# Routed experts in a graph network: edge rows gathered in sixteen blocks by destination, and shares of 13 of 25 node tiles made beside the experts

## The chip, the cores and the metric

The kernel runs on one core of a Trainium2 chip. A core has five engines with a queue each: PE (TensorE, matrix products), DVE (VectorE, elementwise work and reductions), ACT (ScalarE, activation functions), POOL (GpSimd, here mostly the issue of gathers and scatters) and SP (SyncE, plain transfers). Each queue runs in order. Sixteen DMA engines carry the transfers. The metric is the time of one execution in microseconds (us), as the median of several. Times inside the execution are counted from the start of the profiled span.

## What is computed

The program is a stack of graph layers on 3125 nodes with 256 features and edge lists of up to 50000 edges. The change lies in one of them, a feed-forward layer of four experts whose gates come from graph attention. Cut to what matters (M nodes, D=256, 4 heads, 4 experts):

```
h = (x @ W_gat).reshape(M, HEADS, NUM_EXPERTS)
src = concatenate([edge_index[0], loops]); dst = concatenate([edge_index[1], loops])
a_src = (h * att_src).sum(-1); a_dst = (h * att_dst).sum(-1)
e = leaky_relu(a_src[src] + a_dst[dst], negative_slope=0.2)
ee = exp(e - segment_max(e, dst)[dst])
alpha = ee / (segment_sum(ee, dst)[dst] + 1e-16)
agg = segment_sum(h[src] * alpha[:, :, None], dst).reshape(M, 16) + b_gat
scores = layernorm(agg).reshape(M, HEADS, NUM_EXPERTS).mean(1)
topk_s, topk_i = top_k(scores, 2); w = softmax(topk_s)
for ei in range(NUM_EXPERTS):
    g = where(topk_i == ei, w, 0).sum(-1)
    out += g[..., None] * (gelu(x @ W1[ei] + b1[ei]) @ W2[ei] + b2[ei])
```

Here the experts need only `x`, while the gates need, for every node, the rows of all nodes that point at it. There are 32768 such edges, and no node has more than 40 of them.

## The kernel before

**Sizes.** The 3125 nodes are padded to 3200, that is 25 tiles of 128, one node to a partition. `GE` is 32768 edges, `GT` = 256 groups of 128, `GK` = 40 rows fetched per node.

**The survey** (`survey`, L63 to L207) runs first. It counts each node's edges (`gcnt`), and where its run in the sorted list of edges begins (`gstart_i`). It sums up faults (`sv_fault`, five columns) to one number, `bad`. The whole body is built twice: with `bad` at 0 the arm with a plan runs, otherwise a general arm. An early stage of the body then sorts the source numbers of the edges by destination into a list in HBM, `gsorted`.

**The layer** (`routed_layer_in_order`, from L1204) does the following.

1. `router_nodes` normalizes the nodes, makes `xt` (the transposed, normalized nodes), `hg` (the 16 values of W_gat) and the two sides `a_src`, `a_dst`. A table `nodes` with 20 numbers per node (4 of `a_src`, 16 of `hg`) goes to HBM by SP (L1219).
2. On POOL's queue, 256 indirect gathers (helper line L236) fetch the 20 numbers of the source of 128 edges each: `ge<-nodes,src_parts`. The list is laid out with 256 consecutive edges to a partition. Eight tiles of 32 gathers each are written back to HBM as the table `edges`, sorted by destination (L1232). A gather here is a DMA that POOL issues.
3. In five parts of five node tiles, `shares` fetches for each node 40 consecutive rows of `edges`, 80 bytes each (`el<-edges,gstart_i`, one gather for a tile of 128 nodes, 410 KB). Then come the arithmetic of the attention on DVE (L1253 to L1271) and one exp on ACT (L1261). Rows beyond a node's own are pushed to minus infinity by the mask `off` (L1257). The results are `gat_num` and `gat_den`. The buffers `el` and `gat_s` are two each.
4. Beside that, `routed_experts` (L1190) runs 4 experts over 7 chunks of columns, six of 512 and one of 128, written (e, c) below with both counted from 0. A chunk has four pairs of `l0f_ph` product (L1200, two passes of k each) and gelu (L1201, ACT). Then `keep` makes the second product `l0f_po` (L576, in `project`; two node tiles to a PSUM tile) and `put` (L1288, DVE), which adds the bias and frees the PSUM tile. Results of experts 1 to 3 go to HBM through SP (L1290).
5. `router_gates` begins with the `ag` tensor_tensor (L1121), which needs every `gat_num`. The gates weigh the experts' results into X, and the next layer follows.

**What sets the order.** The body is written as a program for a scheduling framework. It puts each engine's instructions in a fixed order and inserts semaphore waits where a tile's or a table's data demand them. `tc.issue_after(x)` puts the instructions within behind x on their engine. `keep` calls `shares(5 * k, put.ins, last.ins)` at the chunks (3,2) to (3,6) of the last expert. DVE's part of the share stands behind the chunk's last `put`, and ACT's exp behind its last gelu. A read of `edges` waits for the writes to it that stand ahead of it, and a later write to it waits for such reads. A tile from a pool of two buffers waits until the one before the last is no longer used.

Of the kernel before, what the change touches and what calls it, by code (L numbers as in the profile page):

```python
# [7 lines left out]
F32 = mybir.dt.float32  # L8
BF16 = mybir.dt.bfloat16
I32 = mybir.dt.int32  # L10
AF = mybir.ActivationFunctionType
OP = mybir.AluOpType
AX = mybir.AxisListType
# [3 lines left out]
P = 128  # L17
N = 3125
NT = 25
# [5 lines left out]
GE = 32768  # L25
GT = GE // P
# [4 lines left out]
NEG = -1.0e30  # L31
# [7 lines left out]
SLOT = P  # L39
GO = 8  # L40
GK = 40


def bcast_rows(ap, width):
# [17 lines left out]
def survey(ctx, tc, A):  # L62
# [9 lines left out]
    with ExitStack() as st:  # L72
# [67 lines left out]
            d0, d1 = WKS.index(k), NT - WKS[::-1].index(k)  # L140
            V.tensor_scalar(first[:, d0:d1], begin[:, d0:d1], row_at[k], None, op0=OP.add)

        fault = sp.tile([P, 5], F32, name="sv_fault")
        V.memset(fault, 0.0)
        V.tensor_tensor(junk, nxt, ids["dst"], op=OP.is_lt)
        V.tensor_reduce(fault[:, 0:1], junk, axis=AX.X, op=OP.max)
        b = sp.tile([P, NT + 1], F32, name="sv_b")
# [42 lines left out]
        V.tensor_tensor(same, far, ids["dst"], op=OP.is_equal)  # L190
        V.scalar_tensor_tensor(same, ids["dst"], float(N), same, op0=OP.is_lt, op1=OP.mult)
        V.tensor_reduce(fault[:, 4:5], same, axis=AX.X, op=OP.max)
        faults = ps.tile([1, 5], F32, name="sv_faults")
        T.matmul(faults, ones[:, :1], fault, start=True, stop=True)
        total = sp.tile([1, 1], F32, name="sv_total")
        V.tensor_reduce(total, faults, axis=AX.X, op=OP.add)
# [13 lines left out]
def body(ctx, tc, A, out, plan):  # L210
# [12 lines left out]
    def load(stack_pool, ap, shape, name, dtype=F32, **kw):  # L223
        t = stack_pool.tile(shape, dtype, name=name, **kw)
        nc.sync.dma_start(t, ap)
        return t
# [8 lines left out]
    def gather(dst, table, idx):  # L235
        return G.indirect_dma_start(out=dst, out_offset=None, in_=table, in_offset=bass.IndirectOffsetOnAxis(ap=idx, axis=0))  # L236
# [967 lines left out]
    def routed_layer_in_order():  # L1204

        with ExitStack() as st:
            open_stage(st)
            sp = pool(st, "l0f")
            gate = sp.tile([P, NT, 4], F32, name="gate")
            ytab = [dram.tile([P, NT, D], F32, name=f"l0f_y{e}") for e in range(4)]  # L1210
            b1 = load(sp, A["l0_ffn_b1"], [P, 16], "l0f_b1")
            with ExitStack() as st2:
                ga = pool(st2, "gat")
                xt, hg, a_src, a_dst = router_nodes(st2, ga)
                node = ga.tile([P, NT, 20], F32, name="node")
                V.tensor_copy(node[:, :, :4], a_src)
                V.tensor_copy(node[:, :, 4:], hg)
                nodes = dram.tile([NP, 20], F32, name="nodes")
                nc.sync.dma_start(nodes[:, :].rearrange("(t p) w -> p t w", p=P), node)  # L1219
                part = load(ga, gsorted[:, :].rearrange("(p j) o -> p (j o)", p=P), [P, GT], "src_parts", I32)  # L1220
                edges = dram.tile([GE + GK, 20], F32, name="edges")
                pad = ga.tile([GK, 20], F32, name="edges_pad")
                V.memset(pad, 0.0)
                nc.sync.dma_start(edges[GE:, :], pad)
                by_part = edges[:GE, :].rearrange("(p j) w -> p j w", p=P)
                gx = pool(st2, "gat_e", 2)
                for j0 in range(0, GT, 32):
                    ge = gx.tile([P, 32, 20], F32, name="ge")
                    for j in range(32):
                        gather(ge[:, j, :], nodes[:, :], part[:, j0 + j : j0 + j + 1])  # L1230

                    G.dma_start(by_part[:, j0 : j0 + 32, :], ge)  # L1232

                num = ga.tile([P, NT, 16], F32, name="gat_num")
                den_ = ga.tile([P, NT, 4], F32, name="gat_den")
                top = ga.tile([P, 5, 4], F32, name="gat_top")


                off = ga.tile([P, NT, GK + 1], F32, name="gat_off")
                V.tensor_tensor(  # L1240
                    off, iota_f[:, None, : GK + 1].to_broadcast([P, NT, GK + 1]), plan["gcnt"][:, :, None].to_broadcast([P, NT, GK + 1]), op=OP.is_ge
                )
                V.tensor_scalar(off, off, NEG, None, op0=OP.mult)
                V.memset(off[:, :, GK:], 0.0)

                def shares(d0, dve, act):

                    el = gx.tile([P, 5, GK + 1, 20], F32, name="el")
                    ds_ = slice(d0, d0 + 5)
                    for i in range(5):  # L1250
                        gather(el[:, i, :GK, :].rearrange("p k w -> p (k w)"), edges[:, :], gstart_i[:, d0 + i : d0 + i + 1])
                    with tc.issue_after(dve):
                        V.tensor_copy(el[:, :, GK, :], node[:, ds_, :])  # L1253
                        s = gx.tile([P, 5, GK + 1, 4], F32, name="gat_s")
                        V.tensor_tensor(s, el[:, :, :, :4], a_dst[:, ds_, None, :].to_broadcast([P, 5, GK + 1, 4]), op=OP.add)
                        V.scalar_tensor_tensor(s, s, 0.2, s, op0=OP.mult, op1=OP.max)
                        V.tensor_tensor(s, s, off[:, ds_, :, None].to_broadcast([P, 5, GK + 1, 4]), op=OP.add)  # L1257
                        V.tensor_reduce(top, s.rearrange("p d k h -> p d h k"), axis=AX.X, op=OP.max)
                        V.tensor_tensor(s, s, top[:, :, None, :].to_broadcast([P, 5, GK + 1, 4]), op=OP.subtract)
                    with tc.issue_after(act):  # L1260
                        S.activation(s, s, AF.Exp)  # L1261
                    V.tensor_reduce(den_[:, ds_, :], s.rearrange("p d k h -> p d h k"), axis=AX.X, op=OP.add)
                    vals = el.rearrange("p d k w -> p (d k) w")[:, :, 4:].rearrange("p e (h c) -> p e h c", h=4)
                    V.tensor_tensor(
                        vals, vals, s.rearrange("p d k h -> p (d k) h")[:, :, :, None].to_broadcast([P, 5 * (GK + 1), 4, 4]), op=OP.mult
                    )

                    for k in (20, 10, 5):
                        V.tensor_tensor(el[:, :, :k, 4:], el[:, :, :k, 4:], el[:, :, k : 2 * k, 4:], op=OP.add)
                    V.tensor_tensor(el[:, :, 0, 4:], el[:, :, 0, 4:], el[:, :, GK, 4:], op=OP.add)  # L1270
                    V.tensor_reduce(num[:, ds_, :], el[:, :, :5, 4:].rearrange("p d k w -> p d w k"), axis=AX.X, op=OP.add)  # L1271


                wp = pool(st2, "l0f_w", 2)
                ps = pool(st2, "l0f_ps", 2, PSUM)
                b2s = {}

                def keep(e, c, cl, ht, w2, last):
                    if e not in b2s:
                        b2s[e] = load(wp, bcast_rows(A["L0_ffn_b2"][e], D), [P, D], "l0f_b2")  # L1280
                    t0, n = c // P, cl // P
                    ys = y_first[:, t0 : t0 + n, :] if e == 0 else wp.tile([P, 4, D], F32, name="l0f_ys")[:, :n]
                    for j in range(0, n, 2):
                        m = min(2, n - j)
                        po = ps.tile([P, 2, D], F32, name="l0f_po")
                        for i in range(m):
                            project(po[:, i, :], ht, w2, j + i)
                        put = V.tensor_tensor(ys[:, j : j + m, :], po[:, :m, :], b2s[e][:, None, :].to_broadcast([P, m, D]), op=OP.add)  # L1288
                    if e:
                        nc.sync.dma_start(ytab[e][:, t0 : t0 + n, :], ys)  # L1290

                    k = c // 512 - 2
                    if e == 3 and k >= 0:
                        shares(5 * k, put.ins, last.ins)

                y_first = stage[0].tile([P, NT, D], F32, name="l0f_y_first", tag="xn")
                routed_experts(wp, ps, b1, xt, keep)
                router_gates(ga, gate, num.rearrange("p t (h c) -> p t h c", h=4), den_)
            with ExitStack() as st2:
                yp = pool(st2, "l0f_yp", 3)  # L1300
                for t in range(NT):
                    V.scalar_tensor_tensor(X[:, t, :], y_first[:, t, :], gate[:, t, :1], X[:, t, :], op0=OP.mult, op1=OP.add)
                for t0 in range(0, NT, 4):
                    n = min(4, NT - t0)
                    for e in range(1, 4):
                        y = yp.tile([P, 4, D], F32, name=f"l0f_yr{e}")
                        nc.sync.dma_start(y[:, :n], ytab[e][:, t0 : t0 + n, :])
                        for j in range(n):
                            t = t0 + j
                            V.scalar_tensor_tensor(X[:, t, :], y[:, j, :], gate[:, t, e : e + 1], X[:, t, :], op0=OP.mult, op1=OP.add)  # L1310
# [954 lines left out]
```

## Time and profile before

| | |
|---|---|
| median of 3 runs | 4866.56 us (4864.06 to 4866.61) |
| profiled execution | 4865.58 us, span 4863.8 us |
| granted PE clock, mean | 0.900 |
| PE, DVE, ACT, POOL busy | 83%, 47%, 24%, 32% of the span |
| first and last `ge` gather issued | 840.56, 1163.28 |
| first `el` gather issued | 1168.93 |
| PE at a standstill | 1143.1 to 1187.69 |
| first share's first sum on DVE | 1178.87 |
| `ag` starts | 1265.67 |

In a line of the timeline the first number is the start, the second the duration, then follow engine, line, operation and operands. In brackets stands how long the engine had been idle before, and which event is taken to have ended that. A line of the waits gives who waited at which line, for whom, the total in us, how often, and the longest. The 25 `el` gathers took:

```profile
L236 POOL DMA_INDIRECT el<-edges,gstart_i x25: 940/942/1770, 1168.9 to 1239.2; - x25
```

The three figures are minimum, median and maximum in ns, then the first and last start in us.

### The profile page before, as it was taken

The page shows a single profiled execution, that of the slowest core. Times are in us where ns is not written, and L with a number is a line of the kernel's source. Part 1 is how long each engine was busy: PE and PEld are TensorE (multiplying, and loading weights), DVE is VectorE, ACT ScalarE, POOL GpSimd, SP SyncE. Part 2 cuts the span into 40 slices and gives each one's busy share as a digit, 9 for nine tenths or more (in the row PEclk, how much of TensorE's full clock was granted, in tenths as well). Part 3 has the DMA queues.
Part 4 walks back from the last instruction along what each step waited for, and adds up shares of the span by engine and source line. Part 5 has one row for each costly group of instructions (what it writes and reads, how often), then busy time and mean ns, then how long its engine had stood idle before and what let it go on. Part 6 is the DMA issues. An engine that isn't in the chain of part 4 may idle for free. (4 is left out here: it accounts for less than half of the span.)

```text
span 4863.8 us, 54448 instructions
## 1 busy us (share of the span) xinstructions
PE 4053.8 (83%) x20057; PEld 2505.6 (52%) x20057; DVE 2280.8 (47%) x6284; ACT 1169.4 (24%) x2820; POOL 1545.1 (32%) x1497
## 2 busy tenths in 40 slices
PE   2488888996099996777689999899999997969987
PEld 2355544664067665555565555444444454634555
DVE  8986443113932337777669997600101033250143
ACT  0167721221021223444312223300102011110021
POOL 2077640775000017777406777200000002200010
PEclk6688889998599997888899999999999998989998
DMA  1046582122523347777614432022221322344200
GB/s 56 10 160 197 192 271 60 39 67 83 168 100 128 133 155 211 206 205 207 188 53 136 149 120 70 3 88 82 70 85 66 95 96 80 91 143 156 82 22 27
DMA packets 286833, 553.40 MB, mean 114 GB/s; under 512 B 81979, under 2 KB 195148, under 8 KB 275676
## 3 DMA queue, kind: packets, MB, share of 16 engines
q1 hardware_dynamic: 215804, 411.42, 25.1%
q0 software_dynamic: 70752, 138.40, 10.7%
q8 instruction: 160, 2.62, 0.2%
q14 instruction: 117, 0.96, 0.1%
HBM read 377.47 MB, written 172.20 MB: 113 GB/s over the span
## 5 line engine op out<-in xcount | busy, mean ns | idle before, releaser
L558 PE MATMUL agg_ps<-tt,h_l 128*128 128x512 bf16 (+3 forms) x3850 | 888.8, 395 | 51.5 <-ACT h_l L2045 44.4
L236 POOL DMA_INDIRECT h_kv<-kv_tab,kv_row x416 | 421.1, 1012 | 189.4 <-issue 65.8
L558 PEld LDWEIGHTS <-h_l 128*128 128x128 bf16 x3150 | 291.5, 98 | 333.4 <-issue 19.5
L239 POOL DMA_INDIRECT wgt_cells<-cw_wsum,cw_to x391 | 392.6, 1004 | 171.1 <-issue 111.6
L239 POOL DMA_INDIRECT gsorted<-gs_i,gpos x256 | 320.4, 1251 | 260.1 <-DVE gpos L909 173.7
L1642 PE MATMUL h_pq<-h_q,h_odt 128*128 128x256 bf16 x1248 | 213.8, 333 | 154.4 <-DVE h_qk L1644 154.2
L236 POOL DMA_INDIRECT ge<-nodes,src_parts x256 | 241.8, 945 | 234.6 <-PE l0f_po L576 156.9
L1842 DVE TENSOR_TENSOR at<-agg_ps,rdeg_r 128x512 f32<-128x512 f32 (+1 forms) x42 | 25.6, 633 | 589.1 <-PE agg_ps L558 589.1
L1962 POOL IOTA trash_slot<- 128x32 f32 x1 | 0.2, 158 | 877.8 <-PE l2g_ph L1861 877.8
L1787 ACT ACTIVATE l1f_h<-l1f_ph,bn_shift,bn_scale 128x512 f32<-128x512 f32 (+1 forms) x224 | 162.7, 731 | 387.2 <-PE l1f_ph L1784 387.2
L1642 PEld LDWEIGHTS <-h_odt 128*128 128x128 bf16 x1248 | 140.8, 116 | 209.8 <-issue 159.1
L558 PEld LDWEIGHTS agg_ps<-tt,h_l 128*128 128x128 f32 x700 | 126.5, 192 | 189.9 <-issue 188.9
L576 PE MATMUL l0f_po<-l0f_w,l0f_ht 128*128 128x256 f32 x800 | 179.8, 382 | 44.6 <-ACT l0f_ht L1201 44.6
L465 PE MATMUL pt<-ident,xn 128*128 128x128 f32 x300 | 64.4, 376 | 180.0 <-DVE xn L456 134.8
L576 PE MATMUL l1f_po<-l1f_Wo,l1f_h 128*128 128x256 f32 x800 | 204.4, 388 | 2.4 <-DVE X L1793 1.2
L1862 ACT ACTIVATE ht_next<-l2g_ph,l_bhid 128x512 f32<-128x512 f32 (+1 forms) x42 | 26.9, 641 | 717.0 <-PE l2g_ph L1861 717.0
L1784 PE MATMUL l1f_ph<-l1f_h,l1f_W 128*128 128x512 f32 (+1 forms) x448 | 195.5, 559 | 1.2 <-ACT l1f_h L1787 0.6
L1693 PE MATMUL h_po<-h_kv,h_of 128*128 128x256 f32 x832 | 189.7, 387 | 7.7 <-DVE h_kv L1689 4.1
L1784 PE MATMUL l1f_ph<-xt,l1f_W 128*128 128x512 f32 (+1 forms) x448 | 191.3, 547 | 1.1 <-issue 1.1
L576 PEld LDWEIGHTS l0f_po<-l0f_w,l0f_ht 128*128 128x128 f32 x800 | 152.9, 192 | 76.2 <-ACT l0f_ht L1201 45.4
L576 PEld LDWEIGHTS l1f_po<-l1f_Wo,l1f_h 128*128 128x128 f32 x800 | 146.1, 190 | 84.3 <-issue 28.3
L1200 PE MATMUL l0f_ph<-xt,l0f_w 128*128 128x512 f32 (+1 forms) x448 | 178.8, 549 | 3.0 <-ACT l0f_ht L1201 2.1
(628 smaller groups left out, 7460.5 us busy)
## 6 DMA issues: line engine op xcount, KB each, us to landing
tt<-cnt_ds SPq DMA_DIRECT2D x90, 640.0 KB
kv_tab<-kv SPq DMA_DIRECT2D x50, 1024.0 KB
tt<-wgt_cells SPq DMA_DIRECT2D x30, 1280.0 KB
wgt_cells<-cw_zero SPq DMA_DIRECT2D x6, 5800.0 KB
cw_row<-cell_r SPq DMA_DIRECT2D x23, 1128.0 KB
cw_ew<-in_ew_r_dram SPq DMA_DIRECT2D x22, 1108.0 KB
cnt_ds<-row_ds SPq DMA_DIRECT2D x150, 128.0 KB
cnt_sd<-cols SPq DMA_DIRECT2D x6, 3200.0 KB
```

Source lines behind the costliest of these rows:

```text
L236: return G.indirect_dma_start(out=dst, out_offset=None, in_=table, in_offset=bass.IndirectOffsetOnAxis(ap=idx, axis=0))
L239: G.indirect_dma_start(out=table, out_offset=bass.IndirectOffsetOnAxis(ap=idx, axis=0), in_=src, in_offset=None, **kw)
L465: T.transpose(pt[:, j, :], src[:, g + j, h * P : (h + 1) * P], ident)
L558: T.matmul(acc[h][:, :width], part[:, s, h * P : (h + 1) * P], tt[:, s - s0, :width], start=(s == 0 and i == 0), stop=(s == NT - 1 and i = ...
L576: T.matmul(psum, lhs[:, i, t * P : (t + 1) * P], rhs[:, i, :], start=(i == 0), stop=(bias is None and i == k - 1))
L1200: T.matmul(ph[:, :cl], w1[:, k, f * P : (f + 1) * P], xt[:, k, c : c + cl], start=(k == 0), stop=(k == 1))
L1642: T.matmul(pq[:, j, :], w["odt"][:, k0 + j, :], w["q3"][:, part, :], start=(part == 0), stop=(part == 2))
L1693: T.matmul(po, of[:, j, :], kv[:, j, D:], start=(k0 + j == 0), stop=(k0 + j == K - 1))
L1784: T.matmul(ph[:, :cl], ws[layer][:, k, o * P : (o + 1) * P], src[:, k, at : at + cl], start=(k == 0), stop=(k == 1))
L1787: S.activation(dst[:, o, :cl], ph[:, :cl], AF.Relu, bias=shi[:, col], scale=sca[:, col])
L1842: V.tensor_tensor(at[:, hf, c : c + cl], psum, rdeg_r[:, c : c + cl], op=OP.mult)
L1862: S.activation(nt_[:, o, c : c + cl], ph[:, :cl], AF.Relu, bias=b_hid[:, o : o + 1])
```

## The change

The 256 groups of edges are divided into `GB` = 16 blocks of 16, each of consecutive destinations: block b holds edges 2048b to 2048b+2047, 16 to a partition. The list of sources is loaded in that layout, in runs of 64 bytes. Each block is written to `edges` on its own (16 writes of 128x320 in place of 8 of 128x640). The node tiles are divided into six parts of 5, 5, 3, 5, 5 and 2 tiles; `GPARTS` gives for each the first tile, the number of tiles, and how many blocks are to be in `edges` before the part's rows are fetched.

A generator, `rows_of_edges`, issues for each part the gathers of its blocks, their writes, and the part's `el` gathers. Two parts are issued ahead of the experts, one more after each call of `shares`. `shares` is called at the chunks (1,4), (2,4), (3,1), (3,4), (3,5) and (3,6).

The table `edges` is filled with zeros first (a memset of 128x1280 and one SP transfer of 2.6 MB). The mask is made for all tiles at once with `a_dst` added in (`off`, 4100 numbers per partition), and each share has one operation less (L1257 is gone). The survey checks that the edges of the first parts do not reach past their blocks: three more columns of faults, three memsets, a matmul, three reductions and one comparison.

```diff
--- before.py
+++ after.py
@@ -39,6 +39,8 @@
 SLOT = P
 GO = 8
 GK = 40
+GB = 16
+GPARTS = [(0, 5, 6), (5, 5, 11), (10, 3, 14), (13, 5, GB), (18, 5, GB), (23, 2, GB)]
 
 
 def bcast_rows(ap, width):
@@ -140,8 +142,11 @@
             d0, d1 = WKS.index(k), NT - WKS[::-1].index(k)
             V.tensor_scalar(first[:, d0:d1], begin[:, d0:d1], row_at[k], None, op0=OP.add)
 
-        fault = sp.tile([P, 5], F32, name="sv_fault")
+        fault = sp.tile([P, 8], F32, name="sv_fault")
         V.memset(fault, 0.0)
+        ready = sp.tile([1, 3], F32, name="sv_ready")
+        for i, (_, _, b) in enumerate(GPARTS[:3]):
+            V.memset(ready[:, i : i + 1], float(b * GE // GB - GK))
         V.tensor_tensor(junk, nxt, ids["dst"], op=OP.is_lt)
         V.tensor_reduce(fault[:, 0:1], junk, axis=AX.X, op=OP.max)
         b = sp.tile([P, NT + 1], F32, name="sv_b")
@@ -190,7 +195,14 @@
         V.tensor_tensor(same, far, ids["dst"], op=OP.is_equal)
         V.scalar_tensor_tensor(same, ids["dst"], float(N), same, op0=OP.is_lt, op1=OP.mult)
         V.tensor_reduce(fault[:, 4:5], same, axis=AX.X, op=OP.max)
-        faults = ps.tile([1, 5], F32, name="sv_faults")
+
+        total_g = ps.tile([1, NT], F32, name="sv_total_g")
+        T.matmul(total_g, ones[:, :1], gcnt, start=True, stop=True)
+        upto_g = sp.tile([1, 3], F32, name="sv_upto_g")
+        for i, (d0, n, _) in enumerate(GPARTS[:3]):
+            V.tensor_reduce(upto_g[:, i : i + 1], total_g[:, : d0 + n], axis=AX.X, op=OP.add)
+        V.tensor_tensor(fault[:1, 5:8], upto_g, ready, op=OP.is_gt)
+        faults = ps.tile([1, 8], F32, name="sv_faults")
         T.matmul(faults, ones[:, :1], fault, start=True, stop=True)
         total = sp.tile([1, 1], F32, name="sv_total")
         V.tensor_reduce(total, faults, axis=AX.X, op=OP.add)
@@ -1217,52 +1229,78 @@
                 V.tensor_copy(node[:, :, 4:], hg)
                 nodes = dram.tile([NP, 20], F32, name="nodes")
                 nc.sync.dma_start(nodes[:, :].rearrange("(t p) w -> p t w", p=P), node)
-                part = load(ga, gsorted[:, :].rearrange("(p j) o -> p (j o)", p=P), [P, GT], "src_parts", I32)
+
+                per = GT // GB
+                part = ga.tile([P, GB, per], I32, name="src_parts")
+                nc.sync.dma_start(part, gsorted[:, :].rearrange("(b p j) o -> p b (j o)", p=P, b=GB))
                 edges = dram.tile([GE + GK, 20], F32, name="edges")
                 pad = ga.tile([GK, 20], F32, name="edges_pad")
                 V.memset(pad, 0.0)
                 nc.sync.dma_start(edges[GE:, :], pad)
-                by_part = edges[:GE, :].rearrange("(p j) w -> p j w", p=P)
+                by_block = edges[:GE, :].rearrange("(b p j) w -> b p j w", p=P, b=GB)
                 gx = pool(st2, "gat_e", 2)
-                for j0 in range(0, GT, 32):
-                    ge = gx.tile([P, 32, 20], F32, name="ge")
-                    for j in range(32):
-                        gather(ge[:, j, :], nodes[:, :], part[:, j0 + j : j0 + j + 1])
-
-                    G.dma_start(by_part[:, j0 : j0 + 32, :], ge)
+                fetched = []
+
+                def rows_of_edges():
+
+                    done = 0
+                    for d0, n, upto_block in GPARTS:
+                        for b in range(done, upto_block):
+                            ge = gx.tile([P, per, 20], F32, name="ge")
+                            for j in range(per):
+                                gather(ge[:, j, :], nodes[:, :], part[:, b, j : j + 1])
+
+                            G.dma_start(by_block[b], ge)
+                        done = upto_block
+                        el = gx.tile([P, 5, GK + 1, 20], F32, name="el")
+                        for d in range(n):
+                            gather(el[:, d, :GK, :].rearrange("p k w -> p (k w)"), edges[:, :], gstart_i[:, d0 + d : d0 + d + 1])
+                        fetched.append(el)
+                        yield
+
+
+                blank = gx.tile([P, 5, GK + 1, 20], F32, name="el").rearrange("p d k w -> p (d k w)")[:, :1280]
+                V.memset(blank, 0.0)
+                nc.sync.dma_start(edges[:GE, :].rearrange("(p a b) w -> p a (b w)", p=P, a=4), blank[:, None, :].to_broadcast([P, 4, 1280]))
+
+                past = gx.tile([P, 5, GK + 1, 20], F32, name="el").rearrange("p d k w -> p (d k w)")[:, : NT * (GK + 1)]
+                past = past.rearrange("p (t k) -> p t k", t=NT)
+                V.tensor_tensor(
+                    past, iota_f[:, None, : GK + 1].to_broadcast([P, NT, GK + 1]), plan["gcnt"][:, :, None].to_broadcast([P, NT, GK + 1]), op=OP.is_ge
+                )
+                V.memset(past[:, :, GK:], 0.0)
+                off = ga.tile([P, NT, GK + 1, 4], F32, name="gat_off")
+                V.tensor_scalar(past, past, NEG, None, op0=OP.mult)
+                V.tensor_tensor(
+                    off, past[:, :, :, None].to_broadcast([P, NT, GK + 1, 4]), a_dst[:, :, None, :].to_broadcast([P, NT, GK + 1, 4]), op=OP.add
+                )
+
+                rows = rows_of_edges()
+                next(rows)
+                next(rows)
 
                 num = ga.tile([P, NT, 16], F32, name="gat_num")
                 den_ = ga.tile([P, NT, 4], F32, name="gat_den")
                 top = ga.tile([P, 5, 4], F32, name="gat_top")
 
-
-                off = ga.tile([P, NT, GK + 1], F32, name="gat_off")
-                V.tensor_tensor(
-                    off, iota_f[:, None, : GK + 1].to_broadcast([P, NT, GK + 1]), plan["gcnt"][:, :, None].to_broadcast([P, NT, GK + 1]), op=OP.is_ge
-                )
-                V.tensor_scalar(off, off, NEG, None, op0=OP.mult)
-                V.memset(off[:, :, GK:], 0.0)
-
-                def shares(d0, dve, act):
-
-                    el = gx.tile([P, 5, GK + 1, 20], F32, name="el")
-                    ds_ = slice(d0, d0 + 5)
-                    for i in range(5):
-                        gather(el[:, i, :GK, :].rearrange("p k w -> p (k w)"), edges[:, :], gstart_i[:, d0 + i : d0 + i + 1])
+                def shares(i, dve, act):
+
+                    d0, n, _ = GPARTS[i]
+                    el = fetched[i][:, :n]
+                    ds_ = slice(d0, d0 + n)
                     with tc.issue_after(dve):
                         V.tensor_copy(el[:, :, GK, :], node[:, ds_, :])
-                        s = gx.tile([P, 5, GK + 1, 4], F32, name="gat_s")
-                        V.tensor_tensor(s, el[:, :, :, :4], a_dst[:, ds_, None, :].to_broadcast([P, 5, GK + 1, 4]), op=OP.add)
+                        s = gx.tile([P, 5, GK + 1, 4], F32, name="gat_s")[:, :n]
+                        V.tensor_tensor(s, el[:, :, :, :4], off[:, ds_], op=OP.add)
                         V.scalar_tensor_tensor(s, s, 0.2, s, op0=OP.mult, op1=OP.max)
-                        V.tensor_tensor(s, s, off[:, ds_, :, None].to_broadcast([P, 5, GK + 1, 4]), op=OP.add)
-                        V.tensor_reduce(top, s.rearrange("p d k h -> p d h k"), axis=AX.X, op=OP.max)
-                        V.tensor_tensor(s, s, top[:, :, None, :].to_broadcast([P, 5, GK + 1, 4]), op=OP.subtract)
+                        V.tensor_reduce(top[:, :n], s.rearrange("p d k h -> p d h k"), axis=AX.X, op=OP.max)
+                        V.tensor_tensor(s, s, top[:, :n, None, :].to_broadcast([P, n, GK + 1, 4]), op=OP.subtract)
                     with tc.issue_after(act):
                         S.activation(s, s, AF.Exp)
                     V.tensor_reduce(den_[:, ds_, :], s.rearrange("p d k h -> p d h k"), axis=AX.X, op=OP.add)
                     vals = el.rearrange("p d k w -> p (d k) w")[:, :, 4:].rearrange("p e (h c) -> p e h c", h=4)
                     V.tensor_tensor(
-                        vals, vals, s.rearrange("p d k h -> p (d k) h")[:, :, :, None].to_broadcast([P, 5 * (GK + 1), 4, 4]), op=OP.mult
+                        vals, vals, s.rearrange("p d k h -> p (d k) h")[:, :, :, None].to_broadcast([P, n * (GK + 1), 4, 4]), op=OP.mult
                     )
 
                     for k in (20, 10, 5):
@@ -1289,9 +1327,10 @@
                     if e:
                         nc.sync.dma_start(ytab[e][:, t0 : t0 + n, :], ys)
 
-                    k = c // 512 - 2
-                    if e == 3 and k >= 0:
-                        shares(5 * k, put.ins, last.ins)
+                    at = [(1, 4), (2, 4), (3, 1), (3, 4), (3, 5), (3, 6)]
+                    if (e, c // 512) in at:
+                        shares(at.index((e, c // 512)), put.ins, last.ins)
+                        next(rows, None)
 
                 y_first = stage[0].tile([P, NT, D], F32, name="l0f_y_first", tag="xn")
                 routed_experts(wp, ps, b1, xt, keep)
```

## Prediction

> **What bounds the kernel now.** I read the tables by stretches first, cut at the layer's own events, to see which engine fills each part of the routed layer.
>
> ```profile
> 1004.00:1091.00 87.00, 86.93 (x316) 58.66 (x315) 8.72 (x13) 18.05 (x29) 66.28 (x72) 1.00 0.27 70
> 1143.00:1188.00 45.00, 0.42 (x2) 0.31 (x2) 8.04 (x7) 2.86 (x3) 26.91 (x29) 0.54 0.35 102
> 1188.00:1230.00 42.00, 36.80 (x138) 25.88 (x137) 39.51 (x37) 13.65 (x18) 10.70 (x10) 0.95 0.41 135
> 1230.00:1266.00 36.00, 0.00 (x0) 0.00 (x0) 32.42 (x32) 4.34 (x4) 4.74 (x5) 0.50 0.23 61
> ```
>
> Columns: stretch, length, then PE, PEld, DVE, ACT and POOL busy (instructions), granted clock, DMA share, GB/s. PE fills the experts (86.93 of 87.00), stands still for 45 us, works again, and ends while DVE has 36 us left. The waits of 831 to 1270 say on what:
>
> ```profile
> ACT gat_s L1261 <- DVE gat_s L1259: 65.0, 4, 44.8
> DVE gat_s L1255 <- DMA el<-edges,gstart_i: 45.2, 1, 45.2
> PE l0f_po L576 <- ACT l0f_ht L1201: 44.6, 1, 44.6
> ```
>
> PE waits for a gelu, the gelu stands on ACT behind the first share's exp, the exp waits for DVE, DVE for the first `el`. The timeline gives each link its moment:
>
> ```profile
> 1163.28 0.94 POOL L236 DMA_INDIRECT ge<-nodes,src_parts  x1 [0.30 <-DMA ge<-nodes,src_parts]
> 1166.19 0.58 POOL L1232 DMA_DIRECT2D edges<-ge  x1 [1.96 <-DMA ge<-nodes,src_parts]
> 1168.93 0.97 POOL L236 DMA_INDIRECT el<-edges,gstart_i  x1 [2.17 <-DMA edges<-ge]
> 1178.87 1.01 DVE L1255 TENSOR_TENSOR gat_s<-el,side_L_ffn_att_dst 128x820 f32<-128x820 f32 x1 [45.18 <-DMA el<-edges,gstart_i]
> 1184.76 0.89 ACT L1261 ACTIVATE gat_s<-gat_s 128x820 f32<-128x820 f32 x1 [44.79 <-DVE gat_s L1259]
> 1187.69 6.37 PE L576 MATMUL l0f_po<-l0f_w,l0f_ht 128*128 128x256 f32 x20 [44.58 <-ACT l0f_ht L1201]
> 1264.76 0.88 DVE L1271 TENSOR_REDUCE gat_num<-el 128x80 f32<-128x400 f32 x1
> 1265.67 0.57 DVE L1121 TENSOR_TENSOR ag<-gat_num,den 128x400 f32<-128x400 f32 x1
> ```
>
> So the layer is bound first by POOL (256 gathers of 0.94 us and a gap of 0.30, from 840.56 to 1163.28), then by DVE: five shares of 15.5 us from 1178.87 to `ag` at 1265.67. My yardstick is the start of `ag`; what follows it is unchanged.
>
> One more reading matters for what is to run side by side:
>
> ```profile
> 1199.22 1.00 DVE L1257 TENSOR_TENSOR gat_s<-gat_s,gat_off 128x820 f32<-128x820 f32 x1
> 1199.57 1.47 POOL L236 DMA_INDIRECT el<-edges,gstart_i  x1 [17.62 <-DVE gat_num L1271]
> 1214.39 1.00 DVE L1255 TENSOR_TENSOR gat_s<-el,side_L_ffn_att_dst 128x820 f32<-128x820 f32 x1
> 1214.74 1.47 POOL L236 DMA_INDIRECT el<-edges,gstart_i  x1 [8.50 <-DVE gat_num L1271]
> 351.26 1.35 DVE L305 TENSOR_TENSOR w_by_rank<-w_rank,iota_b 128x2304 bf16<-128x2304 bf16 x1
> 351.28 7.07 POOL L239 DMA_INDIRECT gsorted<-gs_i,gpos  x1 [0.30 <-issue]
> ```
>
> A gather issued inside a DVE tensor_tensor ends 0.82 us after that operation does: 1199.22+1.00 is 1200.22, and the gather ends at 1201.04; 1214.39+1.00 is 1215.39, and it ends at 1216.21. It was held for what was left of it. The scatter of 351.28 was held through a whole run of such operations. Beside reductions and beside `put` (L1288, one input from PSUM) gathers keep their 0.94.
>
> **The change, part by part.** The built order of instructions, compared on each engine, decides more here than the diff. POOL: 6 blocks, five `el` gathers, 5 blocks, five `el`, then all of the last 5 blocks' 80 gathers, and only then part 2's three `el`. The source reads as if part 2 came after block 14; it is built behind all 256 gathers and ten `el` gathers. ACT: part 2's exp stands after the second gelu of (3,2), where expert 3's chunks are (3,0) to (3,6). DVE: share 3 stands behind the last `put` of (3,4).
>
> Ahead of POOL's start (840.56). The survey gets three memsets, a matmul, three reductions and a comparison. Its matmul and reductions follow `gcnt` (60.84), beside work that ends with `sv_many` at 61.22; the comparison and longer sum stay, I take +0.35 (bounds 0 and 1). The blank's memset on DVE, 128x1280, about 1.1 us by L1438's 0.91 for 1024 elements, stands ahead of the X additions; these are PE-paced, so most is covered; bn operations move behind the last X addition: I take +0.6 (0 to 1.5). Together +1.0.
>
> POOL to part 2. 256+10 gathers at 1.248 are 332.0, 14 edge writes at 0.64 are 9.0: 840.56+1.0+341.0 = 1182.5. The ten `el` gathers moved ahead cost 12.5 of this, six more writes 3.8. The two waits of before (1.96 and 2.17) drop out, since 28 gathers part the last needed write from `el`.
>
> POOL held by shares 0 and 1, which now run on DVE beside these gathers. Both fall in their stretch: share 0's `el` lands near 985, share 1's near 1099. Gathers come every 1.25 us. Of a share's operations those with two SBUF inputs hold: L1255 and L1256 of 1.0 each, L1259 of 1.0, L1264 of 3.56, L1269 of 1.82, 0.98 and 0.57. Between dependent operations the held gather gets in and the next comes 1.25 later. A gather caught evenly spread in L1264 loses 3.56 less half a period, 2.9; the next is caught 1.25 into the 1.82 fold and loses 0.6; then 0.35; the three short ones lose some 0.9 together. That is 4.7 a share; puts between the folds let some in, so I take 4.5, and 9.0 for two. No row shows a gather caught in L1264 or a fold. Lower bound: the mean of the four seen catches (0.83, 0.53, 0.21, 0.53) is 0.53, four a share, 4.2 for two. Upper: two thirds of the 10.2 us of such operations, 14 for two. I am near the middle since holding followed the operation's length in every row. First `el` of part 2: 1191.5.
>
> The Trainium skill, "SBUF — State Buffer", section "SBUF: two separate sides", says that a DVE operation with two SBUF inputs and a GpSimd operation lock each other out entirely. By it DVE would also lose up to 0.94 to each gather it meets; here L1257 took 1.08 beside a gather at 1216.51, against 1.00 at 1199.22. By the rule shares 0 and 1 would be some microseconds longer, which ends nowhere.
>
> Landing. Before, the first five took 9.94 from issue to L1255. Three need 2.5 of issue to the last one against 5.0, so 7.4 (5.0 if the 4.9 behind the last issue halve too, 9.9 if nothing shrinks): 1198.9.
>
> Share 2 to PE. L1255, L1256, L1258, L1259 on 3/5 of the elements: 0.6 of 4.61 is 2.8, 0.15 of gaps, exp 0.53, table load 1.28, gelu 0.69: 5.5. PE resumes at 1204.4, 16.7 later than before.
>
> PE then has 28 passes of (3,2) at 0.215 (6.0), 2.0 lost to the half clock (20 passes took 6.37 after the stall, not 4.3), and two chunks of 13.77: 1239.9. DVE lies idle through most of that, though parts 3 and 4 have landed.
>
> DVE's tail. The share's `off` addition is gone (1.0): 14.5 for five tiles, 5.8 for two and about 1.0 more in gaps: 35.8; three puts 1.8, den and reciprocal 1.0, exps waited for 1.9, less 1.4 of overlap: 39.1. `ag` starts at 1279.0, or +13.4.
>
> Edits at nothing. Zero fill: 2.6 MB on SP's queue at about 787, 12.7 us at the 206 GB/s of the page's busy slices, done before the normalized tiles and the first edges write at 865; without that cover it delays POOL by what is left. `off` of 4100 elements: 4.5 by L1264's rate, on DVE from about 834, when DVE has nothing until 842.42; if later than 840.56 it would hold the first gather. Indices in 64-byte runs: issued near 789, needed at 840. Extra exp table loads: 1.28 twice on ACT beside PE, and a PE wait at (2,5) of some 20 us for share 1. That pushes expert 3 to its stop near 1150, still 54 ahead of 1204, so it costs nothing unless part 2 comes earlier.
>
> Sum: 4865.58+13.4 = 4879.0. The profiled execution (span 4863.8) lies 0.98 under the median of the runs, so 4880.
>
> **Rivals.** What a measurement tells from no change is about 0.2%, 9.7 us: under 4856.8 is faster, over 4876.3 slower.
>
> Not held (same): if holding costs POOL only what was seen, 0 to 4.2, the sum is 4.8 to 9 smaller: 4871 to 4875. For it: the trace has only short catches. Against: in each the wait followed the DVE operation.
>
> Faster: part 2 fetched in the source's turn, after block 14. Then its first `el` is at 1191.5 less 32 gathers (40), about 1151; PE stops only till 1164, (3,4) ends at 1200, the last parts land at 1206, `ag` at 1245: 4847. For it: 36 us of DVE alone are there to be hidden. Against: POOL's queue is in order, and built otherwise. It decides if part 2 lands before about 1176.
>
> Much slower: part 2's landing, or POOL held for whole shares, 14 or more: 4885 to 4893; each microsecond passes to the end one to one, as PE, then DVE's tail, hang on it.
>
> That the survey sends the layer to its other arm: the edges to tiles 0 to 4, 0 to 9 and 0 to 12 number 10178, 20420 and 26582 in the inputs, under the bounds 12248, 22488 and 28632, so the new faults stay 0. I give it nothing.
>
> **How the numbers follow.** Forecast (over 4876) 0.50, much slower 0.10, not held 0.27, faster 0.13. The likeliest one's own range is 4874 to 4886; the whole one, with both ends, 4858 to 4890. Faster 0.13, same 0.27, slower 0.60.
>
> **What would show it.** The first `el` of part 2 near 1191; gathers of 2 to 4 us on POOL beside L1264's successor in shares 0 and 1, some 9 us in sum; PE restarting near 1204; DVE idle some 30 us until (3,4) ends; `ag` near 1279. I am wrong if gathers stay at 0.94 through both shares, if share 3 starts ahead of (3,4)'s last put, or if `ag` comes before 1265.

## The result, and the profile after

The changed kernel takes 4879.11 us (median of 9 runs, 4876.34 to 4885.1), beside 4866.61 for the kernel before in the same runs: a ratio of 1.0025, 95% interval 1.0016 to 1.0034. A second set gave 4878.59 and a ratio of 1.0028 (1.0017 to 1.0040). The change costs 12 to 13 us.

The stretches of the changed kernel, cut at the same events as before (start and end, length, then PE, PEld, DVE, ACT and POOL busy with their instructions, granted clock, DMA share, GB/s):

```profile
1143.00:1204.70 61.70, 11.05 (x36) 6.38 (x34) 6.00 (x9) 5.26 (x7) 42.33 (x47) 0.63 0.20 44
1204.70:1241.00 36.30, 36.27 (x123) 25.30 (x124) 7.75 (x12) 6.05 (x9) 9.57 (x9) 0.93 0.44 141
1241.00:1280.00 39.00, 17.55 (x72) 12.04 (x70) 36.75 (x43) 11.49 (x15) 2.41 (x2) 0.76 0.15 52
```

PE stands still from 1154.05 to 1204.73, where it had resumed at 1187.69 in the kernel before. Then it is full for 36 us in which DVE has 7.75 us of work, and then DVE is busy for 36.75 of 39 us. In the waits (total in us, times, longest) the chain of names is the one of before, only longer:

```profile
ACT gat_s L1299 <- DVE gat_s L1297: 87.4, 6, 50.7
DVE gat_s L1294 <- DMA el<-edges,gstart_i: 74.1, 2, 52.2
PE l0f_po L588 <- ACT l0f_ht L1213: 72.6, 2, 50.7
```

One of PE's two waits is new: 21.9 us for share 1 at (2,5). The timeline from POOL's last gather of edges to `ag`:

```profile
1190.56 0.94 POOL L248 DMA_INDIRECT ge<-nodes,src_parts  x1 [0.30 <-issue]
1191.81 0.94 POOL L248 DMA_INDIRECT el<-edges,gstart_i  x1 [0.30 <-issue]
...
1198.90 0.67 DVE L1294 TENSOR_TENSOR gat_s<-el,gat_off 128x492 f32<-128x492 f32 x1 [52.16 <-DMA el<-edges,gstart_i]
1202.06 0.61 ACT L1299 ACTIVATE gat_s<-gat_s 128x492 f32<-128x492 f32 x1 [50.71 <-DVE gat_s L1297]
1204.73 8.46 PE L588 MATMUL l0f_po<-l0f_w,l0f_ht 128*128 128x256 f32 x26 [50.68 <-ACT l0f_ht L1213]
...
1240.77 0.69 DVE L1326 TENSOR_TENSOR l0f_ys<-l0f_po,l0f_b 128x512 f32<-128x512 f32 x1 [2.76 <-PE l0f_po L588]
1241.66 1.01 DVE L1294 TENSOR_TENSOR gat_s<-el,gat_off 128x820 f32<-128x820 f32 x1
...
1279.97 0.57 DVE L1133 TENSOR_TENSOR ag<-gat_num,den 128x400 f32<-128x400 f32 x1
```

Each step of the predicted chain has its line here. Part 2's first `el` follows the last of all 256 gathers, at 1191.81. Its rows are there at 1198.90, the exp runs at 1202.06, PE resumes at 1204.73. The last `put` of (3,4) is at 1240.77, and share 3 follows within a microsecond, although its five `el` gathers had been issued by 1209.51. `ag` starts at 1279.97.

And the long products of shares 0 and 1 (L1302), with POOL instructions issued beside them:

```profile
998.01 3.56 DVE L1302 TENSOR_TENSOR el<-el,gat_s 128x3280 f32<-128x3280 f32 x1
998.83 0.59 POOL L1253 DMA_DIRECT2D edges<-ge  x1
999.72 2.70 POOL L248 DMA_INDIRECT ge<-nodes,src_parts  x1 [0.30 <-issue]
...
1106.66 3.56 DVE L1302 TENSOR_TENSOR el<-el,gat_s 128x3280 f32<-128x3280 f32 x1
1107.84 3.20 POOL L248 DMA_INDIRECT ge<-nodes,src_parts  x1 [0.30 <-DMA ge<-nodes,src_parts]
```

The gather issued 1.7 us into the first product takes 2.70 us in place of 0.94; the one issued 1.2 us into the second takes 3.20. Both end about 0.8 us after the product does. The `edges` write at 998.83, inside the same product, is not held: it takes its usual 0.59.

### The profile page after: what moved, and what is told of

Its sections match the earlier page's. It is cut to its first block, busy times and chain, and to the rows that moved or that the text cites. A ratio compares the mean times of both kernels' runs of the same rounds, so it can differ in the third digit from the quotient of the medians.

```text
span 4883.3 us, 54409 instructions
## 1 busy us (share of the span) xinstructions
PE 4059.6 (83%) x19975; PEld 2511.3 (51%) x20059; DVE 2285.1 (47%) x6300; ACT 1173.2 (24%) x2823; POOL 1555.9 (32%) x1505
## 5 line engine op out<-in xcount | busy, mean ns | idle before, releaser
L1732 PEld LDWEIGHTS h_po<-h_kv,h_of 128*128 128x128 f32 x832 | 163.2, 199 | 32.6 <-DVE h_kv L1728 5.0
```

The lines of the kernel that those rows point to most:

```text
L1732: T.matmul(po, of[:, j, :], kv[:, j, D:], start=(k0 + j == 0), stop=(k0 + j == K - 1))
```

## The experiments

Each kernel is the changed one with the edit shown. Line numbers are each kernel's own.

**Shares 3 to 5 called earlier.**

```diff
-at = [(1, 4), (2, 4), (3, 1), (3, 4), (3, 5), (3, 6)]
+at = [(1, 4), (2, 4), (3, 1), (3, 2), (3, 3), (3, 4)]
```

> The changed kernel with shares 3, 4 and 5 called at (3,2), (3,3) and (3,4) in place of (3,4), (3,5) and (3,6). Theory (DVE's tail starts only behind the last put of (3,4), though the rows are there by about 1215): part 2 and PE's restart stay at 1192 and 1205, share 3 starts near 1215 in place of 1241.66, PE stops some 5 us more at (3,3), and ag comes at 1254 to 1260, so 20 to 26 us under the changed kernel, 4853 to 4859, under the kernel before. Rival (the late parts wait for freed buffers and PE for the exps, so that PE's last chunks set the end): ag at 1268 or later, 4867 or more.

Measured: 4851.4 us beside 4867.75 for the kernel before, ratio 0.9967 (0.9955 to 0.9980). From its timeline, PE's restart, share 3's first sum, and `ag`:

```profile
1203.58 8.90 PE L588 MATMUL l0f_po<-l0f_w,l0f_ht 128*128 128x256 f32 x26 [50.05 <-ACT l0f_ht L1213]
1213.71 1.01 DVE L1294 TENSOR_TENSOR gat_s<-el,gat_off 128x820 f32<-128x820 f32 x1 [0.34 <-DMA el<-edges,gstart_i]
...
1254.59 0.57 DVE L1133 TENSOR_TENSOR ag<-gat_num,den 128x400 f32<-128x400 f32 x1
```

PE restarts where it did, and share 3 starts as soon as its rows are there (it waited 0.34 us for them), 28 us earlier than in the changed kernel. `ag` is 25.4 us earlier. The stop of some 5 us that was expected of PE at (3,3) did not come: PE waited 0.39 there. DVE's idle time ahead of (3,4)'s last `put` was the place where the loss could be taken back. This version is faster than both kernels, than the one before by 16 us.

**Part 2 fetched in the source's turn.** The gathers of blocks 14 and 15 are ordered behind part 2's `el` gathers.

```diff
-for j in range(per):
-    gather(ge[:, j, :], nodes[:, :], part[:, b, j : j + 1])
+with tc.issue_after(fetch.ins) if b >= 14 else ExitStack():
+    for j in range(per):
+        gather(ge[:, j, :], nodes[:, :], part[:, b, j : j + 1])
...
-    gather(el[:, d, :GK, :].rearrange("p k w -> p (k w)"), ...)
+    fetch = gather(el[:, d, :GK, :].rearrange("p k w -> p (k w)"), ...)
```

> The changed kernel with the gathers of blocks 14 and 15 ordered behind part 2's three el gathers on POOL, as the source reads. Theory (part 2's place in POOL's queue sets PE's restart): part 2's first el at about 1156 in place of 1191.8 (32 gathers earlier, 4 us given back to waits for the writes), PE restarts near 1169 in place of 1204.7, the last parts land near 1216 and become the next bound, ag at 1250 to 1262, time 4849 to 4861. Rival (what is left on DVE and PE behind the gathers sets the end, whatever part 2 does): ag within 3 us of 1280, time 4876 to 4882.

Measured: 4857.18 us, ratio to the kernel before 0.9979 (0.9970 to 0.9988). Its timeline, with part 2's first `el`, PE's restart, the last parts' first `el`, share 3 and `ag`:

```profile
1156.01 0.97 POOL L248 DMA_INDIRECT el<-edges,gstart_i  x1 [2.25 <-DMA edges<-ge]
1169.21 7.57 PE L588 MATMUL l0f_po<-l0f_w,l0f_ht 128*128 128x256 f32 x26 [14.91 <-ACT l0f_ht L1213]
...
1206.80 0.97 POOL L248 DMA_INDIRECT el<-edges,gstart_i  x1 [2.27 <-DMA edges<-ge]
1217.69 1.01 DVE L1295 TENSOR_TENSOR gat_s<-el,gat_off 128x820 f32<-128x820 f32 x1 [12.47 <-DMA el<-edges,gstart_i]
...
1257.70 0.57 DVE L1133 TENSOR_TENSOR ag<-gat_num,den 128x400 f32<-128x400 f32 x1
```

Part 2 comes at 1156.01 and PE restarts at 1169.21. So part 2's place behind all gathers is what held PE in the changed kernel. The end gains only 22 of the 35.5 us by which PE restarts earlier: the last parts' rows are there at 1217.69, and DVE's last 40 us start then. They are the next bound. PE's wait is for share 2's exp on ACT; no run moved that exp to another place, so whether PE could be freed in that way too is not shown.

**Without the long operations of shares 0 and 1.** The multiplication and the folds are left out for the first ten node tiles; one small product in their place keeps the order.

```diff
-V.tensor_tensor(vals, vals, ...)
-for k in (20, 10, 5):
-    ...
+if i >= 2:
+    V.tensor_tensor(vals, vals, ...)
+    ...
+else:
+    V.tensor_tensor(el[:, :, 0, 4:8], el[:, :, 0, 4:8], s[:, :, 0, :], op=OP.mult)
```

> The changed kernel without the multiplication by the shares and the folds (L1302 to L1308) in shares 0 and 1, where only four columns are multiplied; POOL's order is the same. Left out: the weighted sums of the first ten node tiles. Theory (POOL is held by DVE operations with two SBUF inputs for as long as they last): the time that gathers lose beside shares 0 and 1 falls from 7.7 us to 1.7 (the short operations L1294 to L1297 stay), part 2's first el comes at about 1186 in place of 1191.8, and the time falls by 6, to 4873. Rival (gathers lose their time to something else that grows when el and ge transfers overlap): first el within 1.5 us of 1191.8, time as the changed kernel's.

Measured: what the gathers beside shares 0 and 1 take over 0.944 each falls from 7.7 us in sum to 1.6. Part 2's first `el`, and `ag`:

```profile
1185.23 0.95 POOL L248 DMA_INDIRECT el<-edges,gstart_i  x1 [0.30 <-issue]
...
1273.36 0.57 DVE L1133 TENSOR_TENSOR ag<-gat_num,den 128x400 f32<-128x400 f32 x1
```

Both are 6.6 us earlier than in the changed kernel; 0.4 of that is POOL's earlier start (842.94 against 843.35). The time is 4875.84, ratio to the kernel before 1.0016 (1.0006 to 1.0025). Against the changed kernel's 1.0025 that is some 4 us, and the intervals overlap: the gain in time is not shown by itself. The mechanism is, by the trace.

**The layout alone.** Five parts of five tiles, all behind the last block, with the shares called where they were before.

```diff
-GPARTS = [(0, 5, 6), (5, 5, 11), (10, 3, 14), (13, 5, GB), (18, 5, GB), (23, 2, GB)]
+GPARTS = [(0, 5, GB), (5, 5, GB), (10, 5, GB), (15, 5, GB), (20, 5, GB)]
...
-at = [(1, 4), (2, 4), (3, 1), (3, 4), (3, 5), (3, 6)]
+at = [(3, 2), (3, 3), (3, 4), (3, 5), (3, 6)]
```

> The changed kernel's layout (16 blocks, zero fill, mask made ahead, survey) with five parts of five tiles that all wait for the last block, and shares called at (3,2) to (3,6) as before. Theory (the layout costs POOL 8 writes of 0.64 and the later start of 2.8, and gives back 1.0 on DVE per share; the rest of the change's loss is from where the shares stand): first el at 1177, ag at 1267 to 1271, time 4867 to 4873, so 1 to 6 over before. Rival (the layout itself makes the loss): ag at 1277 or later, time 4877 or more.

Measured: 4867.71 us, ratio to the kernel before 1.0000 (0.9991 to 1.0009). First `el`, first share, `ag`:

```profile
1175.93 0.97 POOL L248 DMA_INDIRECT el<-edges,gstart_i  x1 [2.25 <-issue]
1186.36 1.01 DVE L1294 TENSOR_TENSOR gat_s<-el,gat_off 128x820 f32<-128x820 f32 x1 [50.73 <-DMA el<-edges,gstart_i]
...
1268.29 0.57 DVE L1133 TENSOR_TENSOR ag<-gat_num,den 128x400 f32<-128x400 f32 x1
```

POOL is 7.0 us later than before at the first `el`, and DVE gives most of it back (five operations of 1.0 less): `ag` is 2.6 us later, which the times don't show. So blocks, zero fill, mask and survey, taken together, do not make the change's loss: what they cost on POOL they give back on DVE.

**All blocks written ahead of part 2, and both edits at once.** Two versions with the early shares: in one, part 2 waits for all 16 blocks (`(10, 3, GB)` in place of `(10, 3, 14)`); in the other it is fetched in turn, by the edit shown above.

> The version with early shares, with part 2 fetched only after all 16 blocks are written (so the last two writes no longer wait for part 2's rows to land, 4.4 and 2.4 us of idle POOL there). Theory (with early shares the last parts' landing on POOL is the bound, no longer PE's restart): part 2's first el 5 us later, near 1195, PE restarts near 1208 in place of 1203.6, but part 3's rows land near 1209 in place of 1213.7; ag at 1250 to 1253 in place of 1254.6, time 4847 to 4851. Rival (PE's restart still passes to the end): ag 4 to 5 later, near 1259, time 4855 to 4857.

> Both edits at once: early shares and part 2's el gathers in turn. Theory (either edit frees the same stretch, and behind both stands the landing of the last 12 tiles' rows): part 3's rows land at 1217.7 as with part 2 in turn alone, PE stands still until then in (3,3), ag at 1257 to 1262, time 4854 to 4862, no better than either alone. Rival (the gains of 28 and 22 us add): ag near 1235, time near 4830.

Both ran in a set where the mean granted clock was 0.84 and the kernel before took 5721.56. The ratios to it are 0.9915 (0.9884 to 0.9945) and 0.9909 (0.9879 to 0.9938). Two stretches of the first one, then a `put` in each of two chunks that follow each other, and then its last gather of edges and its first share:

```profile
1100.00:1250.00 150.00, 32.49 (x71) 17.01 (x71) 1.38 (x2) 2.75 (x4) 108.39 (x118) 0.58 0.19 40
1250.00:1450.00 200.00, 98.94 (x322) 62.73 (x322) 10.10 (x15) 20.02 (x31) 69.69 (x76) 0.72 0.11 26
```

```profile
1139.76 0.69 DVE L1326 TENSOR_TENSOR l0f_y_first<-l0f_po,l0f_b 128x512 f32<-128x512 f32 x1 [88.91 <-remote]
...
1274.16 0.69 DVE L1326 TENSOR_TENSOR l0f_y_first<-l0f_po,l0f_b 128x512 f32<-128x512 f32 x1 [88.90 <-remote]
...
1354.17 0.94 POOL L248 DMA_INDIRECT ge<-nodes,src_parts  x1 [0.47 <-issue]
...
1458.36 1.01 DVE L1294 TENSOR_TENSOR gat_s<-el,gat_off 128x820 f32<-128x820 f32 x1
```

PE fell behind POOL there: POOL issued its last gather of edges 104 us ahead of share 0, and no wait for rows is left that could tell the theories apart. The granted clock, 0.58 and 0.72 in these stretches, does not explain this by itself. The two `put`s are 134.4 us apart, where a chunk takes 13.8 in the changed kernel at 0.90, and the record shows no clock under 0.5. It shows 0.50 also where PE merely has nothing to do, as from 1230 to 1266 in the kernel before. What made PE ten times slower in these chunks is open. Both versions once more:

> The version with all 16 blocks written ahead of part 2, once more, because the first try ran at a mean granted clock of 0.84, where PE bounded the experts. At the clock of the other runs (0.90), theory (with early shares the last parts' landing is the bound): part 2's first el near 1195, part 3's rows land near 1209, ag at 1250 to 1253, time 4847 to 4851. Rival (PE's restart still passes to the end): ag near 1259, time 4855 to 4857.

> Both edits at once, early shares and part 2's el gathers in turn, once more at the clock of the other runs. Theory: the landing of the last 12 tiles' rows stands behind both, part 3's rows land at 1217.7, ag at 1257 to 1262, time 4854 to 4862, no better than either alone. Rival (the gains add): ag near 1235, time near 4830.

These ran at 0.84 too, beside 5756.05 for the kernel before, with ratios of 0.9947 (0.9926 to 0.9969) and 0.9938 (0.9915 to 0.9961). Whether either beats the early shares alone at a clock of 0.90, and whether the two gains add there, stays open. Both versions are 0.5 to 0.9% faster than the kernel before where PE is that slow; which of their edits does it there is not shown.

**Reductions in place of the long operations.** As the version without the long operations, with two reductions over 3200 numbers added in shares 0 and 1.

```diff
+for _ in range(2):
+    V.tensor_reduce(num[:, ds_, :], el[:, :, :GK, 4:].rearrange("p d k w -> p d w k"), axis=AX.X, op=OP.add)
```

> As the version without the long operations, but in their place two reductions over 3200 numbers in shares 0 and 1 (one input, in a row with the one that is there), which keep DVE as busy as before or busier. Left out: the weighted sums of the first ten node tiles. Theory (what holds POOL is the second SBUF input, not a busy DVE): gathers lose 1.6 us beside shares 0 and 1, as without the long operations, and part 2's first el comes at about 1185. Rival (any long DVE operation holds POOL): they lose 8 us or more, first el at 1191 or later.

> Two long reductions in place of the operations left out in shares 0 and 1, once more, since at the lower clock shares 0 and 1 came after the last gather and nothing was beside them. Left out: the weighted sums of the first ten node tiles. Theory (the second SBUF input holds POOL, not a busy DVE): gathers lose 1.6 us beside shares 0 and 1, part 2's first el near 1185. Rival (any long DVE operation holds POOL): 8 us or more, first el at 1191 or later.

These ran at 0.84 as well, one run each: 5712.77 and 5757.68, beside 5721.56 and 5756.05. The last gather of edges was issued at 1360.96 and 1378.63, and share 0 began only at 1465.55 and 1483.36. So no gather of edges was beside the shares, and the two runs say nothing on holding.

**Operations of three kinds beside the gathers.** To have the answer at any clock, the operations were put into expert 0:

```diff
+if (e, c // 512) in [(0, 1), (0, 3), (0, 5)]:
+    flat = off.rearrange("p t k h -> p (t k h)")
+    with tc.issue_after(put.ins):
+        for i in range(3):
+            if c // 512 == 1:
+                V.tensor_tensor(flat, flat, flat, op=OP.max)
+            elif c // 512 == 3:
+                V.tensor_reduce(spare[:, i : i + 1], flat, axis=AX.X, op=OP.max)
+            else:
+                V.tensor_scalar(flat, flat, 1.0, None, op0=OP.mult)
```

> The changed kernel with nine more operations on DVE in expert 0, beside the gathers and far from the shares: after chunk (0,1) three times off = max(off, off) over 4100 numbers (two SBUF inputs, which leaves off as it is), after (0,3) three reductions of off (one input), after (0,5) three times off * 1 (one input, written back). Theory (the second SBUF input holds POOL for the length of the operation): beside each of the three maxima of about 4.4 us one gather takes up to 4.4 us more and ends 0.8 us after the operation, some 9 us lost in all; beside the reductions, which are longer, and beside the products by 1 gathers keep 0.94 us. Rival (any long DVE operation holds POOL): gathers beside the reductions are held as well. The Trainium skill's page on SBUF names a further case, 2-port operations with one input; by it the products by 1 would hold too.

The clock was 0.90 here. The three groups on DVE, each with gathers that were issued beside it:

```profile
860.96 13.35 DVE L1336 TENSOR_TENSOR gat_off<-gat_off 128x4100 f32<-128x4100 f32 x3
861.81 4.39 POOL L248 DMA_INDIRECT ge<-nodes,src_parts  x1 [0.31 <-DMA ge<-nodes,src_parts]
866.50 4.16 POOL L248 DMA_INDIRECT ge<-nodes,src_parts  x1 [0.30 <-issue]
...
888.51 13.08 DVE L1338 TENSOR_REDUCE gat_spare<-gat_off 128x1 f32<-128x4100 f32 x3
889.80 0.94 POOL L248 DMA_INDIRECT ge<-nodes,src_parts  x1 [0.30 <-DMA ge<-nodes,src_parts]
...
916.06 4.72 DVE L1340 TENSOR_SCALAR gat_off<-gat_off 128x4100 f32<-128x4100 f32 x2
916.63 4.27 POOL L248 DMA_INDIRECT ge<-nodes,src_parts  x1 [0.30 <-issue]
...
920.89 2.54 POOL L1253 DMA_DIRECT2D edges<-ge  x1
921.03 2.29 DVE L1340 TENSOR_SCALAR gat_off<-gat_off 128x4100 f32<-128x4100 f32 x1
```

Beside the maxima (two inputs) three gathers took 4.39, 4.16 and 4.16, and each ended 0.82 us after an operation. Beside 13.08 us of reductions, as busy and with one input, gathers keep 0.94. So the first half of the theory holds, and the rival falls. The theory's second half fails: the products by 1 have one input, and they held a gather to 4.27 and the `edges` write behind it to 2.54. They hold in another way than the maxima: the gather sat through two of them and ended 0.12 us after the second. In sum POOL lost 15.2 us. In a profile of the changed kernel from the same set, part 2's first `el` stood at 1189.35 and `ag` at 1276.55. Here they stood at 1204.93 and 1293.82, 15.6 and 17.3 later, and the time was 4893.42 beside 4878.59, one run against a median. POOL's lateness passes to the end about one to one.

The changed kernel itself was in that set:

> The changed kernel itself, beside the kernel before on the chip of this call. Theory: the loss is made by POOL being later than PE. Where PE has the clock of the first runs (0.90), the changed kernel is 11 to 15 us slower than before, 0.25%. Where the granted clock is 0.84 as in the two last calls, PE bounds the experts, shares 0 to 2 cost the end nothing, and what is left is that ag follows (3,4) by 39 us in place of (3,2) by 87 us, two chunks of 13.8 earlier: the changed kernel is about 20 us faster than before, 0.2% to 0.5%. Rival (the changed kernel is slower by its layout and its place in POOL's queue whatever the clock): slower by 0.2% there too.

It ran at 0.90: 4878.59, ratio 1.0028, as the first branch has it. What the changed kernel does at 0.84 was not measured.

## Why the prediction was right

**What bounds the layer.** The chain of POOL, part 2's rows, share 2's exp, PE, DVE's tail, each waiting for the one before, is shown from two sides. Fetching part 2 earlier moved PE's restart by 35 us. Calling the shares earlier moved `ag` by 25 with the restart in place.

**POOL's start.** Forecast 1.0 later, measured 2.8 (843.35) in the profiled run. Other runs with the same start had 841.67 to 843.39, so 1.1 to 2.8 against the one profile of before: the term was somewhat small. In the profiled run 2.1 us of it were there before the blank's memset began (the last x2t product at 777.72 against 775.61), 0.5 of them from the survey; where the rest comes from is open.

**Holding.** Forecast 9.0, measured 7.7 (3.5 beside share 0, 4.2 beside share 1). The size was off in the product of 3.56 us: 2.9 was put on it, 1.76 and 2.26 were lost. What POOL can still do when the product begins goes by first: a gather under way runs to its end, an `edges` write passes, and so do the gaps of 0.30. The first fold was sized right (0.58 and 0.61 against 0.6). That holding is a cause rests on two runs: 6.1 us of it went with the long operations, and 15.2 came with others put in. The rival in which gathers are hardly held fell with that.

**Landing and share 2.** The rows landed in 7.1 us against 7.4, and PE followed them by 5.8 against 5.5. PE's restart was forecast at 1204.4 and is at 1204.73. The two misses ahead of it, +1.8 and -1.3, nearly cancel: the agreement is better than the terms deserve.

**From PE to the end.** 36.0 us to (3,4)'s last `put` against 35.5, then 39.2 to `ag` against 39.1. The yardstick `ag` moved by 14.3 where 13.4 was forecast, and the medians by 12.5. The profiled execution itself took 4885.1, the longest of the nine, and 5.2 us more than before from `ag` to the end of its span. In the second profile POOL started 1.1 later, lost 7.0 to holding, and `ag` moved by only 10.9, while 1.8 us came behind it. So the prediction was wrong in one place, that nothing changes behind `ag`. In the second profile that place made up for most of the 2.5 us by which `ag` moved less than forecast, and this is luck. What makes the difference there is open.

**The edits at nothing.** Zero fill, indices and mask cost nothing that the times of the layout alone show. The stop of 21.9 us at (2,5) cost nothing either: PE still waited 50.7 us for part 2 behind it.

**The faster rival.** Its mechanism is real: with part 2 in turn the kernel is faster than before. Its size was off by 10 (4847 forecast, 4857.18 measured), since the last parts' rows were there at 1217.69 and not at 1206. The forecast of this rival left out the waits that this order makes on POOL (1.98 and 2.25 at part 2, 2.24 and 2.27 at the last write), share 2's holding of the last gathers (1.7), and one more microsecond of landing.

## What to carry to other kernels

Work that is fetched ahead helps only as far as what stands behind it in each queue is placed to use it: here the order built for POOL put part 2 behind every gather, and the place of the later shares on DVE gave the rest away. One line of call positions turned a loss of 12 us into a gain of 16. Before long elementwise work is put beside a stream of gathers that sets the end, add up the time by which it will hold those gathers.

## What the runs showed of the hardware

A gather that POOL issues inside certain DVE operations waits for them. Inside an f32 tensor_tensor with both inputs in SBUF, of 0.67 to 4.43 us, it ends about 0.8 us after the operation, close to the 0.94 that a free gather takes. A tensor_scalar with one input, 2.3 us over 4100 numbers, holds it too, which I had not expected: there the gather ended 0.12 us after the second of two such operations, so the gap of 0.03 between them had not been enough for it. Reductions of 4.4 us do not hold gathers. A plain write issued by POOL passed a tensor_tensor in 0.59 us, and took 2.54 beside the tensor_scalar. The Trainium skill, "SBUF — State Buffer", section "SBUF: two separate sides", names two such cases: a 2-port mode, and two SBUF inputs, the latter only against a GpSimd operation that reads SBUF, a condition that the prediction left out. The runs fit: a gather reads its indices from SBUF and is held by both, the write is held by one. That the tensor_scalar ran in a 2-port mode they show only so far as it is twice as fast per number as the maxima. The page also has the engine that comes first block the other entirely; of that the runs show one direction, for the maxima took 4.42 to 4.43 us each beside gathers, and a sum over 4100 numbers 4.43 with POOL idle.

Which engine bounds this stage was not the same in all sets of runs. Where the mean granted clock was 0.84, PE took 134.4 us for a chunk that takes 13.8 at 0.90, so it was behind POOL, and the wait that decides everything at 0.90 was gone. The recorded clock alone, never under 0.5 there, does not account for a factor of ten.
